# A graph network on one core: stationary sides spread over twelve slots, an activation in halves, and background steps put off by an estimated list of VectorE

## The chip, the cores and the metric

The kernel runs on one core of a Trainium2 chip. The metric is the device time of one execution in microseconds (us); lower is better. The engines are named as the profile names them: PE is TensorE (matmuls), PEld its weight loads, DVE is VectorE, ACT is ScalarE, POOL is GpSimd, and SP is SyncE, which issues all DMAs here. Each engine works through its own instructions in order.

## The reference

There are 16 graphs of 1024 nodes with 64 channels, and a 0/1 adjacency matrix for each. Four layers follow each other; after each the result is added to its input and normalized. Only the first is unusual, and nearly all of the kernel's time goes to it:

```python
def reference(x, adj, nodemask, ...):
    # layer 0
    nb = (adj_ > 0) & (~eye)                  # neighbours of each node
    rank = jnp.cumsum(nb, axis=-1) - 1
    removed = nb & do_dil & ((rank + 1) % skip == 0)   # "dilation": some edges go
    adj_d = jnp.where(removed | removed.T, 0.0, adj_)
    # for each node and channel: weighted 0.25, 0.5 and 0.75 quantiles
    # (linearly interpolated) over the values of the node's neighbours
    agg = _weighted_nanquantile_agg(x, adj_d > 0)
    y = relu((x + agg) @ W1 + b1) @ W2 + b2
    x = _layernorm(x + y * mask)
    # layer 1: three rounds of relu(norm(adj.T @ (h @ W[l]) + b[l] + h))
    # layer 2: (A @ x) / column sums @ Wn + x @ Ws + bias
    # layer 3: ((A + I) @ x) / row sums
    # each is followed by x = _layernorm(x + layer(x))
```

The sort that the quantiles need is not done per node. The kernel sorts each channel once and finds, for each node, where in the sorted order its quantile lies, by counting neighbours with matmuls.

## The kernel before, in words

**The main loop.** Work is cut into units. A unit is one graph, one of 8 groups of channels (`gr`) and one half (`h`) of 512 nodes, so that there are 16 x 8 x 2 = 256 units. Each unit has S = 6 slots; `y` counts all 1536 slots of the program, `z` the 96 slots of a graph, `p` the 12 slots of a period of two units (one group of channels). A slot is written out in two halves, and `place = 2 * z + half` counts the 192 halves of a graph.

In a slot PE gets, in this order: the matmuls of `words` (tile `pw`), `ranks` (`pr_`), `steps` (`pv`), and in every second slot `sums` (`fc`), each for an older step of a unit; then, in each half, background steps, a part of the next group's stationary sides, and a twelfth of the 68 counting steps of the unit after the current one. DVE gets `masks` for the next step first (`mt`, a comparison, and `pr`, a product), then what the background steps bring. `mt` has 4 buffers, so that DVE's comparison waits for the `pv` matmuls that read the oldest one. The loop also runs `weigh` (`wv`) and `total` (`p8`, `s8`) once per unit or period.

**Counting** (`counts`). For each of KC = 4 sets of a group, 8 matmuls `x1`, 8 matmuls `x2`, and one more onto `x1`, all with 512 columns. ACT moves the results to `cc` and `dw`. Three halves of a slot hold one set. The matmuls' stationary sides are the tile `xw`, four sets for each group.

**Stationary sides** (`word_part`, `word_end`). A set has two sides (`xi`). For each side `word_part` is called twice: four matmuls of 128 columns from `prows` and `words_by` into a bank `pa`, and one activation of 512 elements to `xw`. Then `word_end` runs one activation over the side's 1024 elements. The banks of `pa`, `x1` and `x2` come from one pool of three, `ps_x`. `load_rows` fetches `prows` on SP at slot `p == 2`, for the period after next. Before the change the parts are made in slots 1 to 8 of the period, one in each half, and `word_end` comes after the counting of the second half; slots 9, 10, 11 and 0 have none.

**Background** (`Spread`). Everything else is written as generators, whose pieces between two `yield`s are steps. A `Spread` lays a given number of steps evenly over places `first` to `end`:

- `sort_pair`: for two graphs at once; 55 compare-and-exchange steps (tile `sv`) in even graphs, then 55 steps that turn the order into ranks (`sr`) and a few more in odd ones;
- `dilate`: the next graph's edges (tiles `sc`, `sk`, `vt`), per block of 128 rows a step with a scan, one with small arithmetic, one with an absolute value on ACT, one that writes `vt`; then transposes (`pq`) and row sums (`pm`);
- `transposed`: 16 transposes of adjacency blocks (`pt` from `ac`) with their column sums;
- `layers`: the dense layers of the graph before, with `along` (matmuls with the adjacency read from DRAM, `a`) and `normalized` (`pc`, `sq`, `var`, `rstd` on POOL, and a product on DVE).

The value that a step yields tells what it needs. A `p` means the only bank of the pool `ps_l`, an `h` that it keeps the bank through the next step, a `v` that DVE frees the bank, so that no other may take it in the next half. `Spread.ready` allows a step when its place is due, `Spread.at` forces all that is left in the last place, and `Spread.late` orders the generators within a place, latest first.

**Order.** `link` ties each PE, DVE and ACT instruction of the loop to the one before it in program order (`Ordered`), so that the order on those engines is that of the Python code. The line of nearly all DVE and ACT instructions is that of the call in `Ordered` (L343), and of PE's matmuls L329 and transposes L326; the tiles' names tell them apart.

Of the kernel before, what the change touches and what calls it, by code (L numbers as in the profile page):

```python
# [20 lines left out]
P = 128  # L21
# [7 lines left out]
S = 6  # L29
# [8 lines left out]
def gnn_stack(  # L38
# [31 lines left out]
    dil = ctx.enter_context(tc.tile_pool(name="dil", bufs=1))  # L70
    big = ctx.enter_context(tc.tile_pool(name="big", bufs=2))
    prod = ctx.enter_context(tc.tile_pool(name="prod", bufs=2))
    wts = ctx.enter_context(tc.tile_pool(name="wts", bufs=5))
    work = ctx.enter_context(tc.tile_pool(name="work", bufs=2))
    lay = ctx.enter_context(tc.tile_pool(name="lay", bufs=1))
    strm = ctx.enter_context(tc.tile_pool(name="strm", bufs=3))
# [242 lines left out]
    def link(engine, ins):  # L319
        ins = getattr(ins, "ins", ins)  # L320
        if engine in before:
            tc.add_manual_dep(ins, before[engine].name, nosync, reason="in order")
        before[engine] = ins
# [7 lines left out]
    class Ordered:  # L331


        on = False

        def __init__(self, engine, name):
            self.engine, self.name = engine, name

        def __getattr__(self, op):
            call = getattr(self.engine, op)  # L340

            def do(*args, **kw):
                ins = call(*args, **kw)  # L343
                if Ordered.on:
                    link(self.name, ins)
                return ins

            return do

    V, A = Ordered(nc.vector, "DVE"), Ordered(nc.scalar, "ACT")  # L350

# [172 lines left out]
    def dilate(g, found):  # L524
# [15 lines left out]
        for t in range(T):  # L540
            sc = dil.tile([P, 2 * N], F16, tag="d", name="sc")
            nb, cum = sc[:, 0:N], sc[:, N : 2 * N]
            q = vt[:, t, :]
            for h in range(2):
                V.tensor_scalar(nb[:, ts(h, HALF)], a[h], 0.0, None, ALU.is_gt)
                A.activation(
                    q[:, ts(h, HALF)], a[h], AF.Copy, accum_out=den[:, h, t : t + 1]
                )
            if t + 1 < T:
                a = block_of(t + 1)  # L550
            V.tensor_tensor(nb[:, ts(t, P)], nb[:, ts(t, P)], offdiag, ALU.mult)

            V.tensor_tensor_scan(cum, nb, nb, 0.0, ALU.add, ALU.max)
            yield
            m = cum[:, N - 1 : N]


            sk = small.tile([P, 5], F32, tag="sk", name="sk")
            V.tensor_scalar(sk[:, 0:1], m, 0.5, 0.5, ALU.add, ALU.mult)
            V.tensor_scalar(sk[:, 0:1], sk[:, 0:1], MAGIC, -MAGIC, ALU.add, ALU.add)  # L560
            V.tensor_scalar(sk[:, 1:2], m, T_THRESH, mk[:, t : t + 1], ALU.is_gt, ALU.mult)
            V.scalar_tensor_tensor(
                sk[:, 2:3], sk[:, 0:1], 1.0, sk[:, 1:2], ALU.add, ALU.mult
            )
            V.tensor_scalar(sk[:, 3:4], sk[:, 2:3], -1.5, 1.5, ALU.mult, ALU.add)
            V.tensor_scalar(sk[:, 4:5], sk[:, 2:3], 0.5, -0.5, ALU.mult, ALU.add)
            yield

            A.activation(q, cum, AF.Abs, bias=sk[:, 3:4])
            yield  # L570
            V.tensor_scalar(q, q, sk[:, 4:5], 0.25, ALU.is_equal, ALU.max)
            V.tensor_tensor(q, q, nb, ALU.mult)
            V.scalar_tensor_tensor(
                q[:, ts(t, P)], ident16, 0.25, q[:, ts(t, P)], ALU.mult, ALU.add
            )
            yield
# [400 lines left out]
    def all_of(gen):  # L977
        for _ in gen:
            pass

    class Spread:


# [5 lines left out]
        taken = False  # L989
        closed = -1  # L990

        def __init__(self, gen, steps, first, end):
            self.gen, self.steps, self.first, self.end, self.done = gen, steps, first, end, 0
            self.next, self.held = "", 0

        def step(self, place):
# [16 lines left out]
        def ready(self, place):  # L1013
            if "h" in self.next:
                return place >= self.held + (2 if "p" in self.next else 1)
            if self.done >= self.steps * (place + 1 - self.first) // (self.end - self.first):
                return False
            return "p" not in self.next or (
                place > Spread.closed and Spread.owner is None and not (
                    "n" in self.next and place % 2  # L1020
                )
            )
# [9 lines left out]
                self.step(place)  # L1032

        def late(self, place):
            if "h" in self.next:
                return self.steps
            return self.steps * (place + 1 - self.first) / (self.end - self.first) - self.done

    SLOTS, n_sort = 2 * G8 * S, len(swaps)
    sorted_, parts, infos = [], [], {}  # L1040
# [40 lines left out]
    for k in range(KC):  # L1081
        words[0][k] = wts.tile([P, 2, T, P], F16, tag="xw", name="xw")
        for part in range(4):
            word_part(0, words[0][k], k, part)
            if part % 2:
                word_end(words[0][k], part // 2)
    load_rows(rows_of(0), 1)
    live = {}

    def unit_of(u):  # L1090
# [10 lines left out]
    for y in range(n_units * S + S):  # L1101
        Ordered.on = y < n_units * S
        u, i = divmod(y, S)
        g, z = divmod(y, SLOTS)
        running = u < n_units
        if running and z == 0:
            infos[g]["aggd"] = dram.tile([C, N], F32, name="aggd")
            atd = dram.tile([T, P, N], F32, name="atd")
            deg = small.tile([P, 3, T], F32, tag="deg", name="deg")
            background = []  # L1110
            Spread.closed = -1
            if g % TURN == 0 and g + TURN < B:
                sorting = sort_of(g // TURN + 1, sorted_)
                background.append(Spread(itertools.islice(sorting, n_sort + 1), n_sort + 1, 0, 176))
            elif g % TURN and g + 1 < B:
                background.append(Spread(sorting, n_sort + 4, 0, 132))
            if g + 1 < B:
                background.append(Spread(dilate(g + 1, parts), 51, 0, 160))
            background.append(Spread(transposed(g, deg, atd), 2 * T + 1, 0, 184))
            infos[g].update(atd=atd, deg=deg)  # L1120

        for lag, what in ((1, "words"), (2, "ranks"), (3, "steps")):
            v, s = divmod(y - lag, S)
            if 0 <= v < n_units:
                getattr(live[v], what)(s)
        v, s = divmod(y - 4, S)
        if 0 <= v < n_units and s % 2:
            live[v].sums(s)
        v, s = divmod(y - 5, S)
        if 0 <= v < n_units and s == S - 1 and all_units[v][2]:  # L1130
            total(infos[all_units[v][0]], all_units[v][1], [wvs.pop(v - 1), wvs.pop(v)])
        q, p = divmod(y, 2 * S)
        nq = q + 1
        if running and p == 2 and nq + 1 < B * G8:
            load_rows(rows_of((nq + 1) // G8), (nq + 1) % G8)

        nu, sixth = divmod(y + 1, S)
        nu += 1
        if sixth == 0 and nu < n_units:
            _, counting = unit_of(nu)  # L1140


        v, s = divmod(y + 1, S)
        if v < n_units:
            live[v].masks(s)
        v, s = divmod(y - 4, S)
        if 0 <= v < n_units and s == S - 1:
            wvs[v] = live[v].weigh()
            del live[v]
        for half in range(2):  # L1150

            if running:
                Spread.taken = False
                place = 2 * z + half
                for b in sorted(background, key=lambda b: -b.late(place)):
                    b.at(place)
                if z == 84 and half and g + 1 < B:
                    info(g + 1)
            if running and nq < B * G8 and 1 <= p < 1 + 2 * KC:
                k, part = divmod(2 * (p - 1) + half, 4)  # L1160
                if part == 0:
                    words.setdefault(nq, {})[k] = wts.tile(
                        [P, 2, T, P], F16, tag="xw", name="xw"
                    )
                word_part(nq, words[nq][k], k, part)
            if nu < n_units:
                n = 2 * sixth + half
                all_of(itertools.islice(counting, 68 * (n + 1) // 12 - 68 * n // 12))
            if running and nq < B * G8 and 1 <= p < 1 + 2 * KC and half:
                word_end(words[nq][k], part // 2)  # L1170
        if nu < n_units and sixth == S - 1:
            all_of(counting)
        if z >= SLOTS - S + 1 and g + 1 < B:
            load_rank(g + 1, z - (SLOTS - S + 1))
        if z == 0 and 0 < g < B:
            load_rank(g, S - 1)
        if z == S - 1 and g < B:
            load_weights(g)
        if z == S - 1 and g:
            m = infos.pop(g - 1)  # L1180
            after = layers(g - 1, m["aggd"], m["atd"], m["least"], m["den"], m["deg"])
            if g < B:
                background.append(Spread(after, 61, 2 * S, 2 * SLOTS - 8))
            else:
                all_of(after)

# [45 lines left out]
```

## Time and profile before

| | |
|---|---|
| median of 3 runs | 9796.28 us (9794.57 to 9800.31) |
| the profiled execution's own time | 9801.43 us |
| its span, first to last instruction | 9799.4 us |
| mean granted TensorE clock | 0.987 |
| PE busy | 9001.1 us, 78913 matmuls |
| DVE busy | 8421.3 us, 9786 instructions |
| ACT busy | 7203.8 us, 12321 instructions |
| POOL busy | 211.8 us |
| DMA | 756.03 MB, mean 77 GB/s |
| `mt`, 128x2048 | 1536 of 1220 ns |
| `pr`, 128x4096 | 1536 of 2292 ns |
| `word_part`'s activation, 128x512 | 2048 of 607 ns |
| `word_end`'s activation, 128x1024 | 1024 of 1063 ns |
| absolute value, 128x1024 | 128 of 1156 ns |

The busy time of an engine is the time in which at least one of its instructions runs; matmuls overlap, each taking 379 ns in the records where the next starts after 216. "Idle" is the time in which an engine ran nothing, and the answer on waits names the instruction whose end let the waiting one go, with the sum in us, the number of waits and the longest.

### The profile page before, as it was taken

How to read it: one execution, taken by the hardware profiler on the slowest of the kernel's cores; microseconds unless marked ns; L12 is line 12 of the kernel's file. 1: busy time of each engine (PE TensorE's matmuls, PEld its weight loads, DVE VectorE, ACT ScalarE, POOL GpSimd, SP SyncE). 2: the span in 40 equal slices, each digit the busy share in tenths (PEclk: the TensorE clock that was granted, in tenths of full speed). 3: DMA queues.
4: the chain of work that ended last, by engine and by line, in shares of the span. 5: the costliest groups of instructions: out<-in, count | busy, mean ns of one | idle time of the engine just before them, and what ended most of it. 6: DMA issues, size and time to landing. Idle time of an engine off the chain costs nothing.

```text
span 9799.4 us, 189926 instructions
## 1 busy us (share of the span) xinstructions
PE 9001.1 (92%) x78913; PEld 3857.7 (39%) x78913; DVE 8421.3 (86%) x9786; ACT 7203.8 (74%) x12321; POOL 211.8 (2%) x131
## 2 busy tenths in 40 slices
PE   0699999999999999999999999999999999999996
PEld 0344444434444444444444344443444434444442
DVE  9899979989798998989889898898979989777663
ACT  0688778777787877777778777877778777787772
POOL 0000000000000000000000000000000000000000
PEclk9999999999999999999999999999999999999997
DMA  3112322232222222222222322222322222222113
GB/s 91 48 44 50 99 73 81 70 87 86 71 88 82 71 92 63 94 79 86 69 82 76 83 89 73 74 88 71 99 73 81 68 86 86 67 74 69 52 62 109
DMA packets 732560, 756.03 MB, mean 77 GB/s; under 512 B 303408, under 2 KB 549680, under 8 KB 731696
## 3 DMA queue, kind: packets, MB, share of 16 engines
q1 hardware_dynamic: 731696, 743.90, 24.9%
q8 instruction: 617, 10.11, 0.4%
q14 instruction: 247, 2.02, 0.1%
HBM read 596.88 MB, written 146.81 MB: 76 GB/s over the span
## 4 chain that ended last, share of the span: by engine, by line
PE 51%; DVE 33%; issue 7%; ACT 5%; DMA 3%; POOL 1%; SPq 0%; DVEq 0%; POOLq 0%; ACTq 0%
PE x L329 21%; DVE pr L343 9%; PE pa L329 8%; DVE mt L343 7%; PE pw L329 7%; PE pv L329 5%; DVE sr L343 5%; PE fc L329 4%; DVE sc L343 3%; DVE sv L343 3%; ACT dw L343 2%; DVE vt L343 1%; PE pt L326 1%; ACT xw L343 1%; DVE m L343 1%
## 5 line engine op out<-in xcount | busy, mean ns | idle before, releaser
L329 PE MATMUL x<-vt,xw 128*128 128x512 f16 x16384 | 4059.1, 382 | 63.5 <-ACT dw L343 41.6
L343 DVE TENSOR_TENSOR pr<-mt,dw 128x4096 f16<-128x4096 f16 x1536 | 3520.5, 2292 | 70.7 <-DVE mt L343 0.5
L343 DVE TENSOR_TENSOR mt<-cc,rB 128x2048 f16<-128x2048 f16 x1536 | 1874.1, 1220 | 955.5 <-PE pv L329 912.6
L329 PEld LDWEIGHTS <-xw 128*128 128x128 f16 x16384 | 1500.3, 98 | 1736.7 <-issue 451.6
L343 ACT ACTIVATE xw<-pa 128x512 f16<-128x512 f32 x2048 | 1225.2, 607 | 632.4 <-PE pa L329 618.0
L343 ACT ACTIVATE dw<-x 128x512 f16<-128x512 f32 x2048 | 1114.1, 598 | 576.0 <-PE x L329 564.6
L343 ACT ACTIVATE qq<-pw,col,icol 128x512 f16<-128x512 f32 x1536 | 1201.4, 782 | 422.4 <-PE pw L329 391.9
L343 ACT ACTIVATE xw<-xw 128x1024 f16<-128x1024 f16 x1024 | 1088.1, 1063 | 8.1
L329 PE MATMUL pw<-pr,red 128*32 128x512 f16 x12288 | 934.4, 381 | 47.0 <-DVE pr L343 46.3
L343 ACT ACTIVATE val<-pv 128x512 f32<-128x512 f32 x1536 | 934.1, 608 | 3.5 <-PE x L329 2.5
L329 PE MATMUL pv<-mt,txw 128*32 128x512 f16 x12288 | 931.3, 379 | 0.2 <-ACT nt L343 0.2
L329 PE MATMUL pa<-words_by,prow 128*128 128x128 f16 x8192 | 806.1, 221 | 134.1 <-DMA prow<-rows 99.1
L329 PEld LDWEIGHTS <-prow 128*128 128x128 f16 x8192 | 570.4, 98 | 881.7 <-issue 687.1
L343 ACT ACTIVATE cc<-x 128x512 f16<-128x512 f32 x1024 | 617.4, 603 | 259.1 <-PE x L329 234.3
L329 PE MATMUL fc<-val,fin 128*32 128x512 f32 x3072 | 789.0, 592 | 0.5 <-ACT val L343 0.5
L329 PE MATMUL pw<-rB,subr 128*32 128x512 f16 x6144 | 617.4, 391 | 0.2
L343 DVE TENSOR_TENSOR sr<-sr 128x512 f16<-128x512 f16 x1336 | 599.1, 477 | 16.6
L329 PE MATMUL pv<-nt,nbig 128*32 128x512 f16 x6144 | 598.4, 379 | 0.0
L343 DVE TENSOR_TENSOR sv<-sv 128x512 f32<-128x512 f32 x880 | 566.5, 685 | 0.0
L329 PEld LDWEIGHTS <-txw 128*32 128x32 f16 x12288 | 330.6, 97 | 336.7 <-issue 5.9
L329 PEld LDWEIGHTS <-subr 128*32 128x32 f16 x6144 | 158.0, 93 | 657.6 <-issue 656.7
L329 PEld LDWEIGHTS <-red 128*32 128x32 f16 x12288 | 327.8, 96 | 225.8 <-issue 65.8
(3283 smaller groups left out, 7981.4 us busy)
## 6 DMA issues: line engine op xcount, KB each, us to landing
a<-adj_dram SPq DMA_DIRECT2D x384, 512.0 KB
a<-atd SPq DMA_DIRECT2D x256, 512.0 KB
da<-adj_dram SPq DMA_DIRECT2D x256, 256.0 KB
ac<-adj_dram SPq DMA_DIRECT2D x256, 256.0 KB
atd<-at SPq DMA_DIRECT2D x256, 256.0 KB
swaps<-m SPq DMA_DIRECT2D x440, 128.0 KB
m<-swaps SPq DMA_DIRECT2D x440, 128.0 KB
rB<-rd SPq DMA_DIRECT2D x96, 256.0 KB
```

The source lines that it names most:

```text
L326: link("PE", nc.tensor.transpose(out, in_, id_))
L329: link("PE", nc.tensor.matmul(*args, **kw))
L343: ins = call(*args, **kw)
```

## The change

Three things are changed.

1. *Stationary sides.* `words_at(place)` replaces the two places that built them. Each group of six halves makes one set: part, part, `word_end`, part, part, `word_end`. Four sets fill the 24 halves of a period. They are begun six halves ahead of the period in which they were made before, and `word_end` now stands ahead of the half's counting. The pool of `xw` has 6 buffers instead of 5. The first six halves' work is done before the loop.
2. *Absolute value.* The activation of `dilate` is done in two halves, each in a step of its own.
3. *Putting off.* `Ordered.count` adds an estimated duration for each DVE instruction of the loop to `Ordered.through`; `Ordered.now` is the place's number times 2900 ns. A step that is due is put off while the estimate is more than 4500 ns ahead, until it is 6 places late. `transposed` is never put off, and steps that keep the bank (`h`) are exempt. Lateness is counted in places and no longer in steps. The generators' numbers of steps and ends change with that.

```diff
-    wts = ctx.enter_context(tc.tile_pool(name="wts", bufs=5))
+    wts = ctx.enter_context(tc.tile_pool(name="wts", bufs=6))
...
     class Ordered:
         on = False
+        now = 0
+        through = 0
...
                 if Ordered.on:
                     link(self.name, ins)
+                    if self.name == "DVE":
+                        self.count(op, args[0])
...
+        def count(self, op, out):
+            n = 1
+            for d in out.shape[1:]:
+                n *= d
+            half = out.dtype in (F16, BF16)
+            ns = dict(tensor_tensor_scan=2.1, scalar_tensor_tensor=1.05).get(op)
+            if ns is None:
+                ns = 0.53 if half else 1.05
+                if op == "tensor_scalar":
+                    ns /= 2
+            Ordered.through = max(Ordered.through, Ordered.now) + 150 + ns * n
...
-            A.activation(q, cum, AF.Abs, bias=sk[:, 3:4])
-            yield
+            for h in range(2):
+                A.activation(
+                    q[:, ts(h, HALF)], cum[:, ts(h, HALF)], AF.Abs, bias=sk[:, 3:4]
+                )
+                yield
...
+    PLACE, BUSY, LATE = 2900, 4500, 6
...
-        def __init__(self, gen, steps, first, end):
+        def __init__(self, gen, steps, first, end, wait=LATE):
             self.gen, self.steps, self.first, self.end, self.done = gen, steps, first, end, 0
+            self.wait = wait
...
         def ready(self, place):
             if "h" in self.next:
                 return place >= self.held + (2 if "p" in self.next else 1)
-            if self.done >= self.steps * (place + 1 - self.first) // (self.end - self.first):
+            late = self.late(place)
+            if late < 0 or (late < self.wait and Ordered.through - Ordered.now > BUSY):
                 return False
...
         def late(self, place):
             if "h" in self.next:
-                return self.steps
-            return self.steps * (place + 1 - self.first) / (self.end - self.first) - self.done
+                return self.end
+            return place + 1 - self.first - (self.done + 1) * (self.end - self.first) / self.steps
...
+    def words_at(place):
+        nq, at = divmod(place + 6, 4 * S)
+        nq += 1
+        k, j = divmod(at, 6)
+        if nq >= B * G8:
+            return
+        if j == 0:
+            words.setdefault(nq, {})[k] = wts.tile([P, 2, T, P], F16, tag="xw", name="xw")
+        xi, j = divmod(j, 3)
+        if j < 2:
+            word_part(nq, words[nq][k], k, 2 * xi + j)
+        else:
+            word_end(words[nq][k], xi)
+
+    for place in range(-6, 0):
+        words_at(place)
...
-                background.append(Spread(sorting, n_sort + 4, 0, 132))
+                background.append(Spread(sorting, n_sort + 7, 0, 144))
             if g + 1 < B:
-                background.append(Spread(dilate(g + 1, parts), 51, 0, 160))
-            background.append(Spread(transposed(g, deg, atd), 2 * T + 1, 0, 184))
+                background.append(Spread(dilate(g + 1, parts), 66, 0, 168))
+            background.append(Spread(transposed(g, deg, atd), 2 * T + 2, 0, 184, 0))
...
                 place = 2 * z + half
+                Ordered.now = (2 * y + half) * PLACE
...
-            if running and nq < B * G8 and 1 <= p < 1 + 2 * KC:
-                k, part = divmod(2 * (p - 1) + half, 4)
...
-                word_part(nq, words[nq][k], k, part)
+            if running:
+                words_at(2 * y + half)
...
-            if running and nq < B * G8 and 1 <= p < 1 + 2 * KC and half:
-                word_end(words[nq][k], part // 2)
...
-                background.append(Spread(after, 61, 2 * S, 2 * SLOTS - 8))
+                background.append(Spread(after, 63, 2 * S, 2 * SLOTS - 4))
```

More of the change, by code (lines that the diff above doesn't have):

```diff
@@ L1158, in gnn_stack @@
                     info(g + 1)
-            if running and nq < B * G8 and 1 <= p < 1 + 2 * KC:
-                k, part = divmod(2 * (p - 1) + half, 4)
[L1161 to L1164, printed above, removed]
-                word_part(nq, words[nq][k], k, part)
+            if running:
+                words_at(2 * y + half)
             if nu < n_units:
```

## The prediction

> **What bounds the kernel now.** I read the page's busy times and its chain first, then a table of stretches, then who waited for whom inside the main loop, then two moments on the timeline. The page:
>
> ```profile
> PE 9001.1 (92%) x78913; PEld 3857.7 (39%) x78913; DVE 8421.3 (86%) x9786; ACT 7203.8 (74%) x12321; POOL 211.8 (2%) x131
> PE 51%; DVE 33%; issue 7%; ACT 5%; DMA 3%; POOL 1%; SPq 0%; DVEq 0%; POOLq 0%; ACTq 0%
> ```
>
> PE is busiest and half of the chain, DVE a third of it. The loop runs from the first `pr` (339.7 us) to the last (9622.6). The table of stretches gives it as a whole, the first four eighths of graph 5, the sixth eighth, and one short stretch (columns: us, busy us of PE, PEld, DVE, ACT, POOL; granted clock, DMA share, GB/s):
>
> ```profile
> 3214.40:3287.00 72.60, 69.34 (x621) 28.92 (x619) 69.02 (x98) 59.82 (x104) 0.00 (x0) 1.00 0.22 51
> 3287.00:3361.80 74.80, 67.14 (x601) 29.38 (x599) 73.12 (x96) 56.35 (x100) 1.68 (x1) 0.98 0.22 68
> 3361.80:3436.40 74.60, 73.37 (x634) 31.38 (x631) 72.50 (x101) 60.83 (x107) 1.68 (x1) 1.00 0.28 90
> 3436.40:3510.20 73.80, 68.73 (x606) 29.15 (x605) 70.24 (x97) 57.06 (x100) 1.64 (x1) 0.98 0.30 100
> 3581.10:3653.00 71.90, 66.58 (x626) 30.30 (x626) 62.83 (x67) 54.68 (x92) 1.68 (x1) 1.00 0.20 60
> 3128.90:3132.30 3.40, 3.39 (x14) 1.65 (x18) 3.37 (x5) 0.84 (x3) 0.00 (x0) 0.55 0.35 110
> 339.70:9622.60 9282.90, 8862.82 (x78356) 3799.80 (x78355) 8122.46 (x9084) 7144.27 (x12219) 197.45 (x112) 0.99 0.25 76
> ```
>
> In the loop PE is idle 9282.9 - 8862.8 = 420 us. That is nearly the whole prize, since the change removes no PE work. In an odd graph's first half DVE is 284.9 of 295.8 us busy (96%) and PE idle 17.2; later DVE has room (62.8 of 71.9). Who ended PE's idle time in the loop:
>
> ```profile
> PE pt L326 <- DVE x L343: 51.5, 14, 4.7
> PE pt L326 <- DVE yn L343: 48.5, 28, 3.2
> PE pw L329 <- DVE pr L343: 46.3, 39, 1.7
> PE pc L329 <- DVE y L343: 41.7, 13, 4.2
> PE x L329 <- ACT dw L343: 41.6, 169, 0.2
> PE pt L326 <- DMA ac<-adj_dram: 35.6, 14, 4.4
> PE pa L329 <- ACT xw L343: 28.8, 45, 1.3
> PE pq L326 <- DVE vt L343: 24.4, 20, 2.1
> ```
>
> With the smaller rows of that answer DVE ends 243 us of it (x 53.7, yn 48.5, pr 46.3, y 41.7, vt 42.8, wv and span 9.9), ACT 129, DMA 36. One of the long ones:
>
> ```profile
> 3124.86 0.68 DVE L343 TENSOR_TENSOR wv<-fc,w 96x512 f32<-96x512 f32 x1
> 3125.47 0.67 DVE L343 TENSOR_REDUCE var<-sq 128x8 f32<-128x512 f32 x1
> 3128.16 0.69 DVE L343 TENSOR_TENSOR x<-pc,rstd 128x512 f32<-128x512 f32 x1 [1.81 <-POOL rstd L788]
> 3128.91 1.11 PE L326 MATMUL pt<-ident,ac 128*128 128x128 f32 x4 [4.70 <-DVE x L343]
> 3129.81 2.30 PE L329 MATMUL x<-vt,xw 128*128 128x512 f16 x5
> ```
>
> A transpose needs the one bank of `ps_l`, which DVE frees only after its list; PE, in order, stands 4.70 us. The five `x` matmuls after it took 2.30 us instead of 1.24: that is the 0.55 clock above. The clock records hold 34 such half-rate windows in the loop (3.4 or 6.8 us, 70 us lost), each behind a wait of about 2 us or more, nearly all on `ps_l`.
>
> **Spreading the stationary sides.** Neither PE matmuls (16 x 4 per group) nor activations (607 and 1063 ns) change in number; ACT's share of 2 x 0.61 + 1.06 = 2.28 us in eight of twelve slots becomes 1.52 in all.
> *Removed:* `word_end`'s 1.06 us no longer falls in every odd half, between evictions and the next `qq`. PE waits `pa` and `x` <- ACT xw, 28.8 + 14.0, and `p` <- ACT qq, 16.4, sum to 59 us. A modelled matmul lasts 379 ns but the next starts after 216, so each wait hides 0.16 us more: about 118 of them, 19 us. Of 78 I take 50 off (0 to 78).
> *Added:* a bank conflict that exists now and doubles.
>
> ```profile
> 1637.25 1.09 ACT L343 ACTIVATE dw<-x 128x512 f16<-128x512 f32 x2
> 1637.38 0.38 PE L329 MATMUL pa<-words_by,prow 128*128 128x128 f16 x4
> 1637.89 1.24 PE L329 MATMUL x<-vt,xw 128*128 128x512 f16 x5
> ```
>
> Four `pa` matmuls issue 56 ns apart, so `x` could start at 1637.60; it starts when the first `dw` eviction frees its bank, 0.29 us late (0.41 in most others I looked at). This needs an odd half right after the `neg16` matmul with a `pa` ahead of `x`. The halves are 1, 7, 13 and 19 of a period's 24; today `pa` exists only in 2 to 17, so 7 and 13 pay (223 such waits of 256). After the change `words_at` puts a part in all four: 256 more waits of 0.29 to 0.41, 74 to 105 us. Where DVE sets the pace (half of the odd graphs) PE would have waited anyway; I take 60 (0 to 105).
> *Moved:* words are begun six halves earlier. The rows for them are still loaded at slot 2, so the lead of that SP transfer falls from 22 halves to 14, about 42 us; SP's longest wait in the loop is 29.9 us (L847). Hidden, with 12 us to spare; beyond it PE would wait for `prow`. The last `word_end` comes three halves (9 us) before its matmul, against 1.06 us of ACT. The sixth buffer costs nothing; no wait for `xw` buffers shows, and lead plus life of a set needs it. Six places of words stand ahead of the first counting: 4 x 0.61 + 2 x 1.06 = 4.6 us on ACT once, taken as 3.
>
> **Absolute value in halves.** The row `vt<-sc,sk` has 1154 ns; two halves, by the 633 ns of `vt<-da` at 128x512, 1266: 0.11 x 128 = 14 us on an engine with 2100 us idle. A shorter block in ACT's list may help PE by as little. Only start-up's chain pays, 8 x 0.11 = 1 us. Each block takes one more place, eight of 168; the dilation's pace (66 in 168 against 51 in 160) makes room.
>
> **Putting steps off.** By the code's own costs masks take 1.24 + 2.32 = 3.56 us a slot, a sort step 1.80, a scan step 3.09 and a graph about 535 us, against 192 x 2.9 = 557. So the list has little slack: an idle list holds 0.66 us after the masks, and a scan and a sort step together pass 4.5. The rule acts then, and `layers`, dilation and sort steps start up to six halves late. It doesn't touch masks, held steps (`var`, the product that frees `ps_l`), `info` or, with wait 0, `transposed`. A step put off takes its SP transfers along (swaps, `da`, the first `a` tiles); SP mostly waits for DVE at them (1787 us on `m`), so a shorter DVE list shortens that too.
> What it can win: DVE's 243 us, 24 hidden in those 145 waits (at 0.16), and the 70 of the clock: 337. What it can't: the masks stand ahead of every held step, and the POOL power with its 1.81 us of idle DVE stays. In the wait shown above a sort step ran ahead of the masks and `pr` and `wv` ahead of `var`; only the first would be put off. Some waits are only moved with the new paces. In odd graphs the rank half of the sort (59 steps) is stretched from 132 places to 144: by place 96 it has 41 instead of 43 steps done at its nominal pace, 39 when put off, so 4 x 1.8 = 7 us leave the crowded half for a later eighth with 9 us of room. That bears on the `pr` waits. No row shows the rule at work; the bounds are -337 and, if forced steps pile up at the ends (the sort's last three steps at place 175, 5.4 us more than today's one, in 7 graphs; transposes at 183), +60. I take some 40% of 337, -130, since about that share of the list ahead of PE's waits can be moved.
>
> The Trainium skill, page "TensorE: Matmul & The Clock Gate", section "What's actually happening", lets the clock halve after an idle window of some 3.4 us; here waits of 2.0 to 2.3 us were followed by such windows as well (that at 3722 us, for one), so the measurement decides. By the page alone shortening the 2 us waits would bring back no clock, and some 25 us of the 130 would fall away.
>
> **Sum.** Against the profiled run's own 9801.4 us (span 9799.4): -50 + 60 + 3 + 1 - 130 = -116, so 9685. The median of the runs is 5 us lower than the profiled run; I keep 9685.
>
> **Rivals.**
> *A, the bank wait decides, slower.* 256 more waits at 0.41 us cost 105; `word_end`'s removal gives only 20, and the put-off steps come back in bunches at places 175 and 183, so that DVE waits fall by 60 and no more, while the layers' chain, started late, meets the transposes anew (+25). -20 + 105 + 4 - 60 + 25 = +54: 9855. It decides as soon as the throttle wins less than about 70 us net, since these three first terms make +89 and 20 us are the bound of what can be told. For: the conflict is periodic and certain. Against: the waits on `ps_l` follow lists the rule shortens. 0.20.
> *B, moved, not removed.* Stalls on `ps_l` sit at fixed slots (82, 90, 44, 13 of a graph) because the order is fixed; a new order gives new ones. -50 + 60 + 4 - 20 = -6: 9795. This also covers a rule that hardly acts, as the list passes 4.5 only at crowded places. 0.12.
> *C, nearly all of it.* DVE's 337 down by 230 and the bank wait hidden: 9560. Against: masks and POOL remain. 0.06.
> The forecast: 0.62.
>
> **How the numbers follow.** A measurement of this kernel tells from no change what exceeds about 0.2%, 20 us. Faster: 0.62 + 0.06 = 0.68. Same: 0.12. Slower: 0.20. The range: the forecast with its bounds goes from about 9580 (throttle -235, bank wait 60) to 9760; it must reach into B and most of A to leave out 2 in 10, so 9575 to 9840.
>
> **What would show it.** Right: `x` waits <- ACT dw grow from 169 to above 350; `pa` <- ACT xw nearly vanish; `pt` and `pc` <- DVE fall from 142 us to about 70; fewer than 34 half-rate windows; DVE's busy time in an odd graph's first half falls below 95%, its sixth eighth rises above 66 us. Wrong: if these waits keep their sum, the throttle did nothing; if PE waits for `prow`, the SP lead was too short; if DVE's idle time on `pv` (912.6 us) grows without PE's idle falling, PE's own issue was all there was.

## The result, and the profile after

The change makes the kernel slower: median 9878.94 us (9871.85 to 9887.39), before 9795.42 us, ratio 1.0085 with a 95% interval of 1.0067 to 1.0102. The forecast was 9685 us, faster by 1.2%, with a range up to 9840.

The page of the changed kernel, to be held against the two lines of before:

```profile
PE 9087.2 (92%) x78913; PEld 3880.2 (39%) x78913; DVE 8420.9 (85%) x9786; ACT 7208.3 (73%) x12449; POOL 205.0 (2%) x131
PE 59%; DVE 27%; issue 6%; ACT 5%; DMA 3%; POOL 1%; SPq 0%; another core or an unknown queue 0%; DVEq 0%; POOLq 0%; ACTq 0%
```

DVE does the same work (8420.9 us against 8421.3), with a smaller share of the chain; PE is busy 86 us longer with the same 78913 matmuls. The table of stretches (us, busy us of PE, PEld, DVE, ACT, POOL; granted clock, DMA share, GB/s) for the eighths of graph 5 that were shown of before, a short stretch, and the loop:

```profile
3238.30:3313.10 74.80, 69.70 (x611) 28.47 (x609) 68.54 (x92) 57.91 (x102) 0.00 (x0) 0.95 0.19 50
3313.10:3387.70 74.60, 69.12 (x580) 29.91 (x582) 68.67 (x90) 58.46 (x105) 2.48 (x1) 0.95 0.14 46
3387.70:3459.40 71.70, 70.94 (x636) 29.92 (x632) 66.68 (x90) 57.41 (x101) 2.48 (x1) 1.00 0.30 102
3459.40:3539.00 79.60, 72.45 (x603) 29.79 (x596) 71.90 (x96) 56.09 (x101) 1.68 (x1) 0.96 0.31 98
3615.90:3691.60 75.70, 67.67 (x627) 30.04 (x627) 70.78 (x86) 54.33 (x90) 3.28 (x2) 0.98 0.13 38
344.20:9708.10 9363.90, 8948.21 (x78340) 3819.84 (x78339) 8122.68 (x9086) 7143.44 (x12333) 190.65 (x112) 0.99 0.25 76
```
```profile
3487.70:3494.50 6.80, 5.65 (x11) 1.08 (x12) 6.04 (x8) 1.54 (x2) 0.00 (x0) 0.50 0.11 27
```

The loop is 81.0 us longer (9363.9 against 9282.9), yet PE's idle time is the same, 415.7 us against 420.1. What grew is busy time, by 85 us, and most of it can be accounted for. The clock records hold 56 half-rate windows instead of 34 and lose 134.8 us instead of 70.0 (+65, of which 57 lie in time in which PE was busy). And 125 more waits on a `dw` eviction hide 0.16 us each under the modelled end of a matmul (+20), against 88 fewer waits of other kinds (-14). So some 20 of the 85 us stay open. DVE's work did move as the paces say: from the odd graph's first three eighths (214.6 to 203.9 us) to the later ones (62.8 to 70.8 in the sixth). But the time did not follow: the first three fell from 222.0 to 221.1 us, the fourth rose from 73.8 to 79.6 and the sixth from 71.9 to 75.7. Odd graphs take about 609 us instead of 593, even ones about 580 instead of 583 (from one graph's first `pr` to the next's, my reading of the trace).

Who ended PE's idle time in the loop (us, times, longest), all rows of 19 us and more:

```profile
PE x L329 <- ACT dw L348: 72.4, 294, 0.2
PE p L329 <- DVE wv L348: 47.0, 22, 2.8
PE x L329 <- ACT cc L348: 42.6, 29, 4.5
PE pw L329 <- DVE pr L348: 37.0, 17, 4.8
PE pa L329 <- ACT xw L348: 34.2, 39, 1.9
PE pq L326 <- DVE vt L348: 33.8, 34, 2.4
PE pt L326 <- DMA ac<-adj_dram: 30.6, 10, 4.3
PE pt L326 <- DVE x L348: 20.2, 13, 3.2
PE pt L326 <- DVE yn L348: 19.9, 7, 2.9
```

The waits that the prediction was after did shrink: `pt` and `pc` on DVE's `x`, `yn` and `y` fell from 141.7 to 40 us, and `pc` has no row left. Others took their place: `p` on `wv` (8.9 before), `x` on `cc` (no row before), `pq` on `vt` (24.4 before). One of them on the timeline of the changed kernel, DVE's list first, then PE:

```profile
3475.01 2.29 DVE L348 TENSOR_TENSOR_SCAN sc<-sc 128x1024 f16<-128x1024 f16 x1
3477.22 0.40 DVE L348 TENSOR_TENSOR sr<-sr 128x512 f16<-128x512 f16 x1
...
3484.65 1.22 DVE L348 TENSOR_TENSOR mt<-cc,rB 128x2048 f16<-128x2048 f16 x1
3485.91 2.29 DVE L348 TENSOR_TENSOR pr<-mt,dw 128x4096 f16<-128x4096 f16 x1
3488.11 0.68 DVE L348 TENSOR_TENSOR wv<-fc,w 96x512 f32<-96x512 f32 x1
...
3485.05 1.04 PE L329 MATMUL p<-wv,fin 96*32 96x512 f32 x2 [0.22 <-ACT qq L348]
3488.85 1.06 PE L329 MATMUL p<-wv,fin 96*32 96x512 f32 x1 [2.75 <-DVE wv L348]
```

A scan, two sort steps and the masks of two slots stand ahead of `wv`, so that it comes late, and PE, which works in order, has nothing else to do before `total`'s matmul. The wait takes 2.75 us of idle, and from within it on the clock is at 0.50 for 6.8 us (the short stretch above). PE is busy for 5.65 us of them and loses half, 2.8 us: the price is paid about twice.

A late step of the dilation reaches PE through ACT as well. Six times in the run ACT stands 6.6 to 7.0 us at a half of the absolute value, because `sk` comes late in DVE's list. ACT's `cc` comes after it, and PE waits 4.0 to 4.5 us for `cc`, each time with 6.8 us at half rate:

```profile
3959.67 0.72 ACT L348 ACTIVATE vt<-sc,sk 128x512 f16<-128x512 f16 x1 [7.03 <-DVE sk L348]
3961.87 0.38 PE L329 MATMUL x<-cc,neg 128*128 128x512 f16 x1 [4.46 <-ACT cc L348]
```

### The profile page after: what moved, and what is told of

It is laid out like the page before. It is cut to its first block, busy times and chain, and to the rows that moved or that the text cites. A ratio compares the mean times of both kernels' runs of the same rounds, so it can differ in the third digit from the quotient of the medians.

```text
span 9885.5 us, 189303 instructions
## 1 busy us (share of the span) xinstructions
PE 9087.2 (92%) x78913; PEld 3880.2 (39%) x78913; DVE 8420.9 (85%) x9786; ACT 7208.3 (73%) x12449; POOL 205.0 (2%) x131
## 4 chain that ended last, share of the span: by engine, by line
PE 59%; DVE 27%; issue 6%; ACT 5%; DMA 3%; POOL 1%; SPq 0%; another core or an unknown queue 0%; DVEq 0%; POOLq 0%; ACTq 0%
PE x L329 25%; PE pa L329 9%; PE pw L329 8%; DVE pr L348 7%; PE pv L329 6%; DVE mt L348 6%; DVE sr L348 5%; PE fc L329 4%; DVE sv L348 2%; DVE sc L348 2%; ACT dw L348 2%; DVE vt L348 1%; PE pt L326 1%; PE p L329 1%; DMA xc<-xs 1%
## 5 line engine op out<-in xcount | busy, mean ns | idle before, releaser
L329 PE MATMUL x<-cc,neg 128*128 128x512 f16 x1024 | 391.5, 382 | 42.7 <-ACT cc L348 42.6
```

The source lines that it names most:

```text
L329: link("PE", nc.tensor.matmul(*args, **kw))
```

## The experiments

Every kernel was timed against the kernel before in the same job, whose median there was 9791 to 9796 us.

**The parts, one at a time.** e1 takes before and adds only `words_at` and the sixth buffer.

```diff
+                words_at(2 * y + half)          # e1, instead of slots 1 to 8
```

> Before, with only the stationary sides spread by words_at and the sixth buffer; order of background steps and the absolute value as before. In the profile of the changed kernel x waited for ACT dw 72.4 us in 294 waits instead of 41.6 us in 169. Theory bank (the spread makes twice as many x matmuls wait for the first dw eviction): slower than before by 50 to 75 us, with about 290 such waits and the odd graphs no worse than the even ones. Theory put-off (the loss of some 15 us in each odd graph comes from background steps that are put off): within 20 us of before.

9804.02 us, ratio 1.0011 (1.0001 to 1.0020). The bank wait (`x` on `dw`) nearly doubled, and its 64 us (38.6 visible, 157 x 0.16 hidden) are nearly paid back by the waits on ACT that went:

```profile
PE x L329 <- ACT dw L343: 80.2, 326, 0.2
```

So the theory of the bank has its mechanism, not its price (50 to 75 us net). e2 is the rest of the change:

```diff
-                words_at(2 * y + half)          # e2: made in slots 1 to 8, as before
```

> The changed kernel, with the stationary sides made as before (slots 1 to 8, five buffers); the absolute value in halves, the paces and the putting off stay. Theory bank: faster than before by 10 to 40 us. Theory put-off: slower than before by 60 to 100 us, odd graphs near 608 us against 593, even ones near 578.

9886.62 us, ratio 1.0093 (1.0077 to 1.0110), odd graphs about 608 us, even ones 583. Without the words the loss is as large, so they have hardly a part in it. e3 moves the words by one half, so that the half after `neg16` holds `word_end` and no `pa`:

```diff
-        nq, at = divmod(place + 6, 4 * S)
+        nq, at = divmod(place + 7, 4 * S)
```

> As e1_words, but words are made one half earlier (seven instead of six halves ahead), so that the half after each neg16 matmul holds word_end and no pa. Theory bank: the x waits on dw fall from 41.6 us (before) to under 10 us, the time lies 60 to 110 us below e1_words and 20 to 60 us below before. Theory put-off: the words do not matter, within 20 us of e1_words.

9715.86 us, ratio 0.9924 (0.9909 to 0.9938). The row `x` <- ACT dw is gone from the answer; 88 us less than e1 for one half's shift, and 76 below before, more than the 20 to 60 expected. e4 never puts a step off:

```diff
-    PLACE, BUSY, LATE = 2900, 4500, 6
+    PLACE, BUSY, LATE = 2900, 10**9, 6
```

> The changed kernel with the limit of the list at 10^9 ns, so that no step is ever put off; words, halves and the new paces stay. Theory put-off: 40 to 80 us below the changed kernel, odd graphs back to about 595 us. Theory bank: within 20 us of the changed kernel. If neither holds and the time rises, the putting off itself helped and the new paces cost.

9689.04 us, ratio 0.9893 (0.9879 to 0.9908): putting steps off costs 190 us, far above the 40 to 80 expected and more than all of the loss, and the remainder of the change is a gain of 1%. e4's fourth, fifth and sixth eighth of graph 5 and its loop, for the table above:

```profile
3401.30:3470.80 69.50, 67.25 (x598) 29.53 (x600) 67.81 (x93) 57.22 (x103) 1.68 (x1) 1.00 0.32 104
3470.80:3541.50 70.70, 69.78 (x616) 29.36 (x605) 68.62 (x85) 53.45 (x92) 1.64 (x1) 1.00 0.32 103
3541.50:3611.10 69.60, 65.17 (x624) 29.90 (x623) 66.22 (x77) 53.50 (x91) 2.49 (x1) 1.00 0.18 50
344.30:9507.10 9162.80, 8853.58 (x78350) 3797.88 (x78351) 8115.71 (x9085) 7142.03 (x12333) 212.19 (x112) 1.00 0.25 77
```

Against e4 the changed kernel's loop is 201 us longer: 106.5 us more idle time of PE (415.7 against 309.2) and 94.6 us more busy time. The clock records lose 92 us more (134.8 against 42.7), 82 of them in busy time. Some of PE's waits in e4, to be held against those of the changed kernel above:

```profile
PE p L329 <- DVE wv L348: 25.0, 16, 2.3
PE pc L329 <- DVE y L348: 18.4, 12, 2.4
PE x L329 <- ACT cc L348: 17.4, 20, 1.0
PE pq L326 <- DVE vt L348: 13.2, 20, 0.9
```

Putting off raised `p` on `wv` (to 47.0), `x` on `cc` (42.6), `pq` on `vt` (33.8), and `pt` on `x` and `yn`, which e4 has for 1.1 us and the changed kernel for 40.1. It lowered `pc` on `y` and `pw` on `pr` (54.8 in e4, 37.0).

**Which step must not be late.** f1, f2 and f3 exempt one generator each (`wait` 0). The last argument of its `Spread` is the edit:

```diff
-                background.append(Spread(dilate(g + 1, parts), 66, 0, 168))
+                background.append(Spread(dilate(g + 1, parts), 66, 0, 168, 0))   # f3
```

> The changed kernel, but layers is never put off (its wait is 0); sort and dilation still are. The changed kernel took 9879 us, without any putting off 9689. Theory layers (their late start sets their bank steps against the dilation's): 60 to 130 us below the changed kernel. Theory sort (what is pushed from the crowded first third of an odd graph lands where dilation and layers already fill DVE): at most 30 us below.

> The changed kernel, but the sort is never put off; layers and dilation still are. Theory sort: 100 to 150 us below the changed kernel, odd graphs near 590 us. Theory layers: at most 40 us below.

> The changed kernel, but the dilation is never put off; sort and layers still are. Theory sort and theory layers: within 40 us of the changed kernel, mostly the DVE waits for the xc transfer at a graph's end change. If it is the dilation's scans and transposes coming late, 60 us or more below.

f1: 9806.14 us (1.0016, 1.0007 to 1.0026). f2: 9794.76 us (1.0006, 0.9997 to 1.0015). f3: 9708.16 us (0.9914, 0.9897 to 0.9930). Neither theory holds through the three: layers took back 73 us, the sort 84, the dilation 171, and the sum, 328, is far above 190. The parts are not independent. j1 turned it round, with the dilation late and the others not:

```diff
+    PLACE, BUSY, LATE = 2900, -10**9, 6      # j1: and wait 0 for sort and layers
```

> The changed kernel with the dilation always 6 places late and sort and layers never late. Theory dilation (its late scans and transposes are what costs): 9820 to 9890. Theory offset (what counts is how the generators, the transposes and weigh lie to each other, and no one of them): between 9700 and 9800, as the other mixtures were.

9795.51 us (1.0005, 0.9995 to 1.0014): late alone it costs 107 us against e4, not 190. Its long waits stand elsewhere (`pc` on `y` up to 6.7 us, `pw` on `pr` up to 6.0).

**How late, and does the list choose?** Three more variants of the same line: the limit at -10^9 (g3, every step 6 places late), 3 places instead of 6 (h1), and 3050 ns for a place (g2).

```diff
+    PLACE, BUSY, LATE = 2900, -10**9, 6     # g3
+    PLACE, BUSY, LATE = 2900, 4500, 3       # h1
+    PLACE, BUSY, LATE = 3050, 4500, 6       # g2
```

> The changed kernel with the limit of the list at -10^9, so that every step but those held and the transposes starts 6 places late, whatever the list. Theory lateness: at or above the changed kernel, 9860 to 9950, in even graphs too (above 590 us). Theory collisions: a uniform shift keeps the even spacing, so 9680 to 9760, odd graphs under 592 us.

> The changed kernel with steps put off by at most 3 places instead of 6. Theory lateness: about half the loss of 190 us, 9770 to 9800. Theory collisions: no such proportion, anywhere from 9690 to 9880, with the odd graphs holding the difference.

> The changed kernel with 3050 ns instead of 2900 for a place, near the 3.05 us that a place takes in the trace, so that the list runs down faster and the rule acts less. Theory collisions (a step put off by a list that does not know who on PE waits lands where it hurts): between 9700 and 9820, in step with how often it acts. Theory lateness (all steps being 6 places late against the fixed ends is what costs): near the changed kernel's 9879 only if the steps are still as late, else lower too.

g3: 9901.04 us (1.0112, 1.0097 to 1.0127). h1: 9825.47 us (1.0035, 1.0021 to 1.0048). g2: 9823.37 us (1.0034, 1.0020 to 1.0048). Lateness as such explains this better than a bad choice by the list, though not every number: g3's even graphs take about 585 us, not above 590, and h1 lies above its 9770 to 9800. The fourth to sixth eighth of graph 5 in g3 show why:

```profile
3468.40:3547.00 78.60, 70.77 (x588) 29.65 (x585) 71.90 (x96) 54.96 (x100) 1.68 (x1) 0.97 0.30 100
3547.00:3623.90 76.90, 74.66 (x637) 31.62 (x636) 69.67 (x90) 58.03 (x101) 0.00 (x0) 0.99 0.31 103
3623.90:3699.60 75.70, 67.69 (x628) 30.47 (x627) 70.77 (x87) 54.31 (x90) 3.27 (x2) 0.98 0.13 38
```

With all steps always late these are the changed kernel's eighths again (79.6, 76.9 and 75.7 us there). In the middle of an odd graph the list is over its limit without a break: the costs of `count`, added up over DVE's instructions in the order of the changed kernel's trace, stand above 4500 ns in both halves of every slot from 9 to 77 of graph 5. So there the rule chooses nothing; it only starts everything 6 places late. The loss is not in proportion either, 136 us for 3 places and 190 for 6.

**Late against what?** j2 is g3 with the transposes late as well, k1 is the changed kernel with one more slot for `wv`:

```diff
+            background.append(Spread(transposed(g, deg, atd), 2 * T + 2, 0, 184))   # j2
-        v, s = divmod(y - 5, S)      # total
+        v, s = divmod(y - 6, S)      # k1
```

> Everything 6 places late, the transposes too. Always 6 late without the transposes took 9901 us. Theory offset against the transposes: 9690 to 9770. Theory offset against weigh and total, or theory lateness against the ends of a graph: 9870 or more.

> The changed kernel with total one slot later (6 slots behind instead of 5), so that PE asks for wv a slot later. Theory offset against weigh: the waits p <- DVE wv and sk (57 us) nearly vanish and with them half of the half-rate windows they cause: 9790 to 9830. Theory lateness against the ends: less than 30 us below 9879.

j2: 9913.59 us (1.0123, 1.0108 to 1.0138), so late transposes do not bring the time back; PE's waits of `pt` on `x` grew instead (139 us, up to 12.2, against 53 in g3). k1: 9780.86 us (0.9990, 0.9981 to 0.9999), 98 us below the changed kernel, with no row of `p` on `wv` or `sk` left among PE's waits. That one slot saved 25 us where nothing is put off (k2 against f4, below). So about 70 of the 190 us go once `total` leaves the late list one slot more. They are not the waits of `p` alone, since `x` on `cc` fell too (42.6 to 24.7 us). The other 120 or so are not taken apart by a run; in the traces they stand as waits of 1 to 5 us on `x` (for `cc`), `pw`, `pq` and `pt`, at slots that differ from variant to variant. All eleven late arrangements (9708 to 9914 us, the changed kernel among them) lie above the 9689 without lateness; why none of them came out well is not settled.

**What made the gain.** g1 has the new paces and the order of generators alone, l1 only the order, with the paces of before:

```diff
-            return self.steps * (place + 1 - self.first) / (self.end - self.first) - self.done
+            return place + 1 - self.first - (self.done + 1) * (self.end - self.first) / self.steps
```

> Before with only the new paces and the lateness counted in places: no putting off (limit 10^9), words in slots 1 to 8 as before, the absolute value in one step (dilation 57 steps in 168, which keeps its end). Without putting off the whole change took 9689 us, and the words alone cost 12 us. If paces and order make the gain: 9670 to 9700. If the gain needs the halves of the absolute value or the even words: 9760 or more.

> Before with only the lateness counted in places (the order in which due steps are written within a place); paces, words, absolute value as before, nothing put off. Theory order: 9670 to 9730, the pt waits on DVE x and yn (100 us before) largely gone. Theory paces: 9770 to 9810, with those waits unchanged.

g1: 9677.07 us (0.9883, 0.9869 to 0.9898). l1: 9674.59 us (0.9879, 0.9863 to 0.9896). It is the order: 117 us by counting lateness in places. The transposes have 17 steps in a graph; counted in steps they were hardly ever the latest, and the last five were written in slots 82, 83, 89, 89 and 91 of graph 5, beside the layers' last products. Counted in places they come first when due (76, 80, 83, 89, 91). PE's waits of before, `pt` on `x` 51.5 and on `yn` 48.5, and the 35.6 on the transfer of `ac`, became in l1:

```profile
PE pt L326 <- DVE yn L348: 26.6, 14, 3.2
PE pt L326 <- DVE x L348: 23.4, 11, 3.8
```

with no row for the transfer, and 23 half-rate windows (49.5 us). So half of the waits on `x` and `yn` went, not nearly all as expected; with the transfer's and the clock's share this makes 106 of the 117 us.

**Versions that beat both.** f4 is e4 with e3's shift, k2 adds k1's later `total`, l2 has order, shift and `total` on the old paces.

> The changed kernel with no putting off (limit 10^9) and words seven halves ahead instead of six. If both findings add: 9689 less the 88 us that seven instead of six saved without the paces, 9590 to 9640, with the x waits on dw under 10 us. If the gains overlap, 9660 or more.

> No putting off, words seven halves ahead, total one slot later: the 9599 us of f4_never7 less its waits p <- DVE wv (31 us) and p <- ACT qq (16 us), 9545 to 9580. If those waits only move, 9590 to 9605.

> l1_order with words seven halves ahead in six buffers and total one slot later; old paces, absolute value in one step, nothing put off. If the gains add: 9675 - 76 (words) - 20 (total) = 9579, so 9555 to 9605. If the paces and halves carry part of k2_best's 9574 us: 9610 or more.

f4: 9599.42 us (0.9802, 0.9788 to 0.9817). k2: 9574.48 us (0.9779, 0.9764 to 0.9794), the fastest. l2: 9613.66 us (0.9810, 0.9794 to 0.9826): with the other two in place, the new paces and the halves together are worth 39 us, though with the order alone the paces were worth nothing (g1 against l1). PE's idle time in the loop of f4 is 266 us, against 420 before.

## Why the prediction was wrong

By the runs the change sums to: order -117 (l1), words +12 (e1), putting off +190 (the changed kernel against e4), and paces and halves +2, which is what remains. 9792 + 87 = 9879. The parts are not independent, as l2 shows for the paces, so another order of adding them could share the 87 out otherwise.

*What bounds the kernel.* Right that PE's issue is the floor and that waits of PE are all there is to gain. Wrong that idle time is nearly the whole prize: from before to after idle time stayed and 65 us came as half-rate clock. The prediction counted the clock's 70 us as something to win; that a moved wait can also add to them it left out.

*Spreading the words.* Predicted -50 + 60 + 3 = +13, measured +12 by itself. That fits in its terms too: the bank wait was forecast at 74 to 105 us gross, taken at 60, and measured at 64; in the changed kernel it grew from 169 waits to 294, under the 350 named. That `pa` <- ACT xw would nearly vanish was wrong there (34.2 us). The lead of SP's `prow` transfer held; PE has no row for it in the loop. That one more half of lead would do away with the conflict (88 us in e3) the prediction did not see.

*Absolute value in halves.* Costed at about nothing. No run has it alone; with the paces it comes out at +2 by the sum above, and in the best versions the two together gained 39 us.

*Putting steps off.* This step failed: -130 forecast, +190 measured (e4), outside its bounds of -337 and +60. The working took the list as a whole, 535 of 557 us, and let the rule act only at crowded places. The 0.66 us that it has after the masks holds for a slot's second half; in the first the masks alone make 3.56 of the 4.5. By the same costs the first 64 slots of an odd graph hold 228 us of masks, 93 of sort and 43 of dilation blocks, 364 of their 64 x 5.8 = 371 before any `pq`, layers or `wv` (a sort step of these graphs is four instructions, 1.69 us, not 1.80). So there the list never runs down, and the rule is a plain delay of 6 places, as g3 shows. The second error is what a delay does. The `ps_l` waits did shrink (`pt` and `pc` on `x`, `yn` and `y` from 142 us to 40, below the 70 named), but not by the rule, and that is luck: without it they are 19.5 us (e4), and the order and the paces brought them down. What the rule moves away from one wait comes ahead of another: `wv`, which the prediction listed with `span` at 9.9 us and never as a place to arrive at, `sk` and through it `cc`, and `pq`. Each costs its time, and the long ones their clock. Two signs of being right came true, DVE at 92% in an odd graph's first half and 70.8 us in the sixth eighth, but DVE's room there was no gain, since PE waits there for single items of that list; the half-rate windows rose to 56 instead of falling. Why every late arrangement costs, beyond the share of `total`, stays open.

*The order within a place.* The prediction did not cost it at all, although the change in `late` was in front of it. It was worth -117 us, the largest gain in the change. By luck it hides a part of the miss: without it the forecast would have been off by some 310 us instead of 194.

*The rivals.* A had the sign, with the bank wait as cause; e1 shows that this is not where the time went, so its 9855 is near by luck. B named the mechanism, stalls moved to other slots, but gave them the same size, where they grew against e4 and halved the clock.

*The clock.* Waits of about 2 us were enough for a half-rate window here. In the changed kernel 41 of the 56 windows have no idle time of PE over 3.4 us beside them, only shorter ones down to 1.6 us; PE has 15 such long waits in all, and the `p` wait above had 2.75 us of idle. The wait at 3722 us that the prediction names lasted 2.91 us, not 2.0 to 2.3; before has three others of 2.0 to 2.1 us with a window. The Trainium skill, page "TensorE: Matmul & The Clock Gate", section "What's actually happening", asks for an idle window of about 3.4 us before the clock halves. The measurement decides.

## What to carry to other kernels

A rule that delays work by an estimated list must be checked for how often it acts: where the estimate is always over its limit it smooths nothing, and a run with the rule always on shows that at once. An engine's free time is no cover for work moved into it while an in-order engine waits for single items of its list; follow each such item (`wv`, the product that frees a bank) and see what will stand ahead of it. When a hand-written order has one bank or buffer shared by slow and fast generators, the unit in which their lateness is compared can be worth more than the pacing.

## What the runs showed of the hardware

How long a wait of PE must be to halve the clock shows in the changed kernel: a half-rate window began in, or within 3.4 us after, none of the 29 waits of 1 to 1.5 us, 8 of the 38 up to 2 us, 29 of the 37 from 2 to 3 us, and all 15 over 3.4 us. Such a wait can cost twice its length, as the one on `wv` did (2.75 us and 2.8 us of clock), but there is no fixed factor: putting off brought 106.5 us more idle time and 92 us more lost to the clock, while from before to e4 idle time fell by 111 us and the loss by only 27. And idle time in a profile whose matmuls overlap hides 0.16 us of every short wait (379 less 216 ns), which made 125 more bank waits look 31 us dear instead of an estimated 51.
